# Filler tiles that put nearly every operand of TensorE at 96 modulo 256 bytes of a partition

## The chip, the cores and the metric

The kernel runs on one core of one Trainium2 chip. The metric is the device time of one execution in microseconds (us), the median of three executions.

## What is computed

The input is 16 sequences of 1024 tokens with 512 features, in float32. Each sequence goes through a linear attention block and a feed-forward block, each with a residual sum and a layer norm behind it. The reference, cut to what matters:

```python
# attention: 16 heads of 32
qkv = x @ Wqkv.T + bqkv
q, k, v = split(qkv);  q = rmsnorm(q, gq);  k = rmsnorm(k, gk)
q, k = apply_rope(q), apply_rope(k)
qf, kf = relu(q), relu(k)
vpad = concatenate([v, ones])
vk   = einsum('bhlp,bhld->bhpd', vpad, kf)      # one matrix for a head of a sequence
res  = einsum('bhpd,bhld->bhlp', vk, qf)
attn = res[..., :-1] / (res[..., -1:] + 1e-6)
x = layernorm(x + rmsnorm(attn @ Wout.T + bout, gout))
# feed-forward: mixes each token with the one before it
xr = mu_r * x + (1 - mu_r) * x_prev;  xk = mu_k * x + (1 - mu_k) * x_prev
out = sigmoid(xr @ W_r.T) * (square(relu(xk @ W_k.T)) @ W_v.T)
x = layernorm(x + out)
```

## The kernel before, in words

Tokens go in tiles of 128 (N = 128 tiles, 8 to a sequence). Every float32 matrix product is made of three products: each operand is split in a rounded high part and the rest (`fp32r` tiles named ...h and ...l), and high by high, high by low and low by high are added up in PSUM. Nearly all of TensorE's instructions are therefore pairs of a weight load of 128 x 128 and a matmul with 512 moving columns. In what follows "moving" is the operand that streams (the `rhs` of the code) and "stationary" the one that the weight load reads (`lhsT`).

**Stage A** (slots `slot(i)`, one for each tile, in the first 1250 us or so). `proj` (line 366 on) makes q and k of tile i into `psq` and `psk`: the moving operand is `wqk_h` or `wqk_l`, the stationary one `xh` or `xl`, 12 matmuls each. `add_kx` (line 449) adds x^T k of the tile before into four PSUM banks `pskx`, 12 matmuls: moving `kh` or `kl`, stationary `xnh` or `xnl`. After the eight tiles of a sequence `finish_a` to `finish_c` turn these sums into four matrices m (`pskv` from `kx` by `wa_h` and `wa_l`, `psks` from the key sum, `psm` from `wout_h`, `wout_l` by `kvth`, `kvtl`), which are stored to DRAM.

**Stage B** (the rest). For each tile: `part_qt` transposes q (`psqt`), `part_m` makes the attention output `psy` (moving `mb`, stationary `qth`, `qtl`), and for each block of four tiles `part_t` transposes x (`pst`) and mixes, `part_fk` makes `psk` (moving `mkh`, `mkl`; stationary `w_k`), `part_fr` makes `psr` (moving `w_r`; stationary `mrh`, `mrl`) and `part_fv` makes `psv` (moving `w_v`; stationary `kah`, `kal`). The products of stage B are all emitted by the helper `product` at line 153, 12 matmuls each; the transposes at line 138 use the identity `ident` as moving operand.

The order of the instructions comes from a scheduler that the tile framework runs over the program. It is the same before and after, on every engine and on the DMA queues, and so are all waits.

**Where a tile lies.** SBUF is divided by pools. Pools on the left side grow upwards: `const` first, then `work`, then the pools of the stages (`consta`, `worka`; later `constb`, `workm`, `workb`, `workr`). Pools with `side="right"` grow downwards from the top: `top` first, below it `end`, `endkx`, `endk`; in stage B `workc` takes their place below `top`. A tile's place is its pool's start plus the sizes of the tiles before it, each rounded up to 32 bytes. Nearly all large tiles have a multiple of 2048 bytes in a partition, so the few small tiles ahead of them set where all of a pool begins modulo 256. The addresses of the built program, modulo 256:

| operand of TensorE | pool | before |
|---|---|---|
| `wqk`, `xh`, `xl`; `qth`, `qtl`; `w_k`, `mkh`, `mkl`, `kah`, `kal`; `w_r`, `mrh`, `mrl` | left pools | 96 |
| `mb`, four buffers of six in its ring | `work` (left) | 96 |
| `mb`, the other two buffers; `w_v` | `workc` (right) | 224 |
| `kh`, `kl`, `xnh`, `xnl`; `kx`, `wa`; `wout`, `m` | `endk`, `endkx`, `end` (right) | 192 |
| `ones`, `kvth`, `kvtl` | `end`, behind `bv` and `mask` (right) | 224 |
| `x` (stationary of `pst`), seven buffers in `top`, four in `workc` | right | 224 |
| `q` (stationary of `psqt`) | `top` (right) | 224 |
| `ident` (moving of `pst`, `psqt`) | `const` (left) | 160 |

Of the kernel before, what the change touches and what calls it, by code (L numbers as in the profile page):

```python
# [8 lines left out]
F32 = mybir.dt.float32  # L9
# [6 lines left out]
P = 128  # L16
DIM = 512
NC_ = DIM // P
# [15 lines left out]
def kernel(  # L34
# [34 lines left out]
    const = ctx.enter_context(tc.tile_pool(name="const", bufs=1))  # L69
# [3 lines left out]
    tp = ctx.enter_context(tc.tile_pool(name="top", bufs=1, side="right"))  # L73
# [27 lines left out]
        return pp.tile([P, DIM], F32, tag="mm", bufs=4, name=name)  # L101


    halo = const.tile([P, NC_], F32, name="halo")
    ident = const.tile([P, P], F32, name="ident")
    make_identity(nc, ident)
# [149 lines left out]
    with ExitStack() as a_ctx:  # L256

        te = a_ctx.enter_context(tc.tile_pool(name="end", bufs=1, side="right"))
# [87 lines left out]
            omm[n] = const.tile([P, NC_], F32, name=f"omm_{n}")  # L346
            V.tensor_scalar(omm[n], mu[n], -1.0, 1.0, ALU.mult, ALU.add)

        bv = te.tile([P, NC_], F32, name="bv")
        with nc.allow_non_contiguous_dma(reason="512 numbers"):  # L350
            nc.scalar.dma_start(
                out=bv, in_=bqkv[2 * DIM : 3 * DIM].rearrange("(g p) -> p g", p=P)
# [526 lines left out]
```

## Time and profile before

| | |
|---|---|
| time, median of 3 executions | 2803.57 us (2799.61 to 2805.04) |
| time of the profiled execution | 2802.45 us |
| its span, first to last instruction | 2800.6 us |
| granted TensorE clock over the span | 0.994 of full |
| TensorE matmuls | 12536, busy 2728.1 us (97%) |
| weight loads | 12536, busy 2236.0 us (80%), beside the matmuls |
| VectorE, ScalarE, GpSimd busy | 79%, 68%, 26% |
| DMA | 431.17 MB, mean 154 GB/s |

[...] The chain of work that ended last shows spacings best: a row "start, us, PE, what, x12" is a run of twelve matmuls with nothing between them, and its time divided by twelve is their mean spacing.

### The profile page before, as it was taken

The page shows a single profiled execution, that of the slowest core. Times are in us where ns is not written, and L with a number is a line of the kernel's source. Part 1 is how long each engine was busy: PE and PEld are TensorE (multiplying, and loading weights), DVE is VectorE, ACT ScalarE, POOL GpSimd, SP SyncE. Part 2 cuts the span into 40 slices and gives each one's busy share as a digit, 9 for nine tenths or more (in the row PEclk, how much of TensorE's full clock was granted, in tenths as well). Part 3 has the DMA queues.
Part 4 walks back from the last instruction along what each step waited for, and adds up shares of the span by engine and source line. Part 5 has one row for each costly group of instructions (what it writes and reads, how often), then busy time and mean ns, then how long its engine had stood idle before and what let it go on. Part 6 is the DMA issues. An engine that isn't in the chain of part 4 may idle for free.

```text
span 2800.6 us, 40329 instructions
## 1 busy us (share of the span) xinstructions
PE 2728.1 (97%) x12536; PEld 2236.0 (80%) x12536; DVE 2201.8 (79%) x4966; ACT 1893.1 (68%) x3839; POOL 735.8 (26%) x808
## 2 busy tenths in 40 slices
PE   7999999999999999988999999999999999999998
PEld 5788877777888888866788888888888888888887
DVE  7988877777888788866778787878787878788774
ACT  5566655555555566655777777777777777777775
POOL 6422221221222222222322222222222222222221
PEclk9999999999999999999999999999999999999999
DMA  7787776666777777755323222232323132313210
GB/s 245 234 294 254 236 256 204 213 209 202 231 237 238 237 230 237 231 176 176 104 70 106 95 77 92 92 110 65 106 91 113 57 113 84 110 65 106 76 57 30
DMA packets 230854, 431.17 MB, mean 154 GB/s; under 512 B 24544, under 2 KB 24800, under 8 KB 230640
## 3 DMA queue, kind: packets, MB, share of 16 engines
q1 hardware_dynamic: 228384, 425.85, 46.9%
q10 hardware_dynamic: 2256, 2.76, 0.3%
q8 instruction: 99, 1.62, 0.2%
q14 instruction: 115, 0.94, 0.1%
HBM read 313.14 MB, written 115.38 MB: 153 GB/s over the span
## 4 chain that ended last, share of the span: by engine, by line
PE 76%; DVE 1%; DMA 1%; ACT 1%; issue 0%; POOL 0%; SPq 0%; POOLq 0%; ACTq 0%; DVEq 0%
PE psk L153 13%; PE psv L153 12%; PE psy L153 12%; PE psr L153 12%; PE pskx L462 7%; PE psq L370 7%; PE psk L370 7%; PE pst L138 2%; PE psqt L138 2%; PE psm L538 1%; PE pskv L505 1%; DMA m_d<-m 0%; DMA w_r<-w_dr 0%; PE pskv L513 0%; DMA mb<-m_d 0%
## 5 line engine op out<-in xcount | busy, mean ns | idle before, releaser
L153 PE MATMUL psk<-mkh,w_k 128*128 128x512 f32 x1024 | 337.3, 396 | 0.0
L153 PE MATMUL psr<-w_r,mrh 128*128 128x512 f32 x1024 | 325.9, 400 | 2.6 <-issue 2.6
L153 PE MATMUL psv<-w_v,kah 128*128 128x512 f32 x1024 | 326.4, 400 | 1.5 <-DVE qtl L209 1.5
L153 PE MATMUL psy<-mb,qth 128*128 128x512 f32 x1024 | 319.8, 393 | 2.3 <-ACT qth L208 1.4
L117 POOL TENSOR_TENSOR rstd_all<-ss,mhalf 128x2 f32<-128x2 f32 x128 | 119.1, 931 | 685.6 <-DVE ss L432 666.7
L245 DVE TENSOR_TENSOR y<-psy,g_out 128x512 f32<-128x512 f32 x128 | 88.5, 691 | 187.3 <-PE psy L153 186.6
L370 PE MATMUL psq<-wqk_h,xh 128*128 128x512 f32 x512 | 204.1, 399 | 26.2 <-ACT psq L132 26.2
L153 PEld LDWEIGHTS psy<-mb,qth 128*128 128x128 f32 x1024 | 192.6, 189 | 46.3 <-ACT qth L208 2.2
L153 PEld LDWEIGHTS psk<-mkh,w_k 128*128 128x128 f32 x1024 | 192.3, 188 | 39.4
L153 PEld LDWEIGHTS psr<-w_r,mrh 128*128 128x128 f32 x1024 | 189.5, 190 | 40.1 <-issue 2.8
L153 PEld LDWEIGHTS psv<-w_v,kah 128*128 128x128 f32 x1024 | 187.9, 188 | 41.9 <-DVE qtl L209 1.9
L649 POOL TENSOR_TENSOR mkl<-mixk,mkh 128x512 fp32r<-128x512 f32 x128 | 175.6, 1372 | 150.2 <-ACT mkh L648 150.2
L462 PE MATMUL pskx<-kl,xnh 128*128 128x512 f32 x512 | 203.1, 397 | 5.6 <-DVE kl L439 5.5
L370 PE MATMUL psq<-wqk_l,xh 128*128 128x512 f32 x512 | 203.8, 398 | 0.0
L370 PE MATMUL psq<-wqk_h,xl 128*128 128x512 f32 x512 | 203.7, 398 | 0.0
L462 PE MATMUL pskx<-kh,xnl 128*128 128x512 f32 x512 | 202.2, 395 | 0.0
L153 PE MATMUL psv<-w_v,kal 128*128 128x512 f32 x512 | 202.1, 395 | 0.0
L370 PE MATMUL psk<-wqk_h,xh 128*128 128x512 f32 x512 | 200.4, 391 | 1.8 <-ACT psk L132 1.8
L153 PE MATMUL psy<-mb,qtl 128*128 128x512 f32 x512 | 201.6, 394 | 0.0
L153 PE MATMUL psr<-w_r,mrl 128*128 128x512 f32 x512 | 201.5, 394 | 0.0
L370 PE MATMUL psk<-wqk_h,xl 128*128 128x512 f32 x512 | 200.2, 391 | 0.0
L370 PE MATMUL psk<-wqk_l,xh 128*128 128x512 f32 x512 | 199.8, 390 | 0.0
(148 smaller groups left out, 7248.9 us busy)
## 6 DMA issues: line engine op xcount, KB each, us to landing
tab<-tab_d SPq DMA_DIRECT2D x480, 256.0 KB
xt<-in_xt_dram SPq DMA_DIRECT2D x128, 256.0 KB
xn<-in_x_dram SPq DMA_DIRECT2D x128, 256.0 KB
q_d<-ro SPq DMA_DIRECT2D x128, 256.0 KB
m_d<-m SPq DMA_DIRECT2D x64, 512.0 KB
mb<-m_d SPq DMA_DIRECT2D x64, 512.0 KB
q<-q_d SPq DMA_DIRECT2D x128, 256.0 KB
x<-in_x_dram SPq DMA_DIRECT2D x128, 256.0 KB
```

Of the source, the lines that this page charges most:

```text
L117: G.tensor_tensor(dst, src, mhalf[:, 0 : src.shape[1]], ALU.pow)
L138: T.matmul(ps[:, n * P : (n + 1) * P], lhsT=b, rhs=ident, is_transpose=True, start=(n == 0), stop=(n == NC_ - 1), skip_group_check=True,)
L153: T.matmul(ps, lhsT=a[u][:, rows], rhs=b[w][:, cols], start=(afresh and c == 0 and k == 0), stop=(c == n - 1 and k == 2), skip_group_check ...
L245: V.tensor_mul(y, ps, g_out)
L370: T.matmul(ps, lhsT=a[i][:, c, :], rhs=w_qk[b][:, c, cols], start=False, stop=(c == NC_ - 1 and n == 2), skip_group_check=True,)
L462: T.matmul(ps_kx[b][c], lhsT=a[:, cols], rhs=r, start=(t == 0 and n == 0), stop=(t == 7 and n == 2),)
L505: T.matmul(ps, lhsT=w_a["h"][:, c, cols], rhs=kx[:, c, g, :, :].rearrange("p two n -> p (two n)"), start=(g % 2 == 0 and c == 0), stop=Fal ...
L538: T.matmul(ps, lhsT=a[:, g, :], rhs=w_o[r][:, g, :], start=(n == 0), stop=(n == 2))
L649: (V if n == "r" and s != 1 else G).tensor_sub(ml, m, f32(mh))
```

## The change

Three tiles change their size or are added; none of the three added stretches is ever read or written. In `const` a tile of 256 bytes stands ahead of all others, in `top` one of 128 bytes, and `bv` in `end` grows from 16 bytes (32 with rounding) to 256.

```diff
@@ -101,6 +101,9 @@
+
+    const.tile([P, 64], F32, name="fill_const")
+    tp.tile([P, 32], F32, name="fill_top")
     halo = const.tile([P, NC_], F32, name="halo")
     ident = const.tile([P, P], F32, name="ident")
@@ -346,7 +349,7 @@
-        bv = te.tile([P, NC_], F32, name="bv")
+        bv = te.tile([P, 64], F32, name="bv")[:, 0:NC_]
```

In the built program every tile on the left moves up by 256 bytes and keeps its residue. The tiles of `top` stay at their addresses: the pool's start moves down by 128 bytes and the filler takes these. The pools below `top` start 128 bytes lower; in `end` the tiles ahead of `bv`, and with them all of `endkx` and `endk`, lie 224 bytes lower still. Modulo 256 the operands of TensorE then stand so:

| operand | before | after |
|---|---|---|
| `kh`, `kl`, `xnh`, `xnl`, `kx`, `wa`, `wout`, `m` | 192 | 96 |
| `ones`, `kvth`, `kvtl` | 224 | 96 |
| `w_v`, the two `mb` buffers and the four `x` buffers of `workc` | 224 | 96 |
| all that stood at 96 | 96 | 96 |
| `ident` | 160 | 160 |
| `q`, the seven `x` buffers of `top` | 224 | 224 |

No instruction, order, wait or transfer is added, removed or moved; only addresses differ.

## The prediction

> **What bounds the kernel now.** I read three views in this order: the busy times by stretch, who TensorE waited for, and the chain of work that ended last.
>
> ```profile
> PE 2728.1 (97%) x12536; PEld 2236.0 (80%) x12536; DVE 2201.8 (79%) x4966; ACT 1893.1 (68%) x3839; POOL 735.8 (26%) x808
> PEclk9999999999999999999999999999999999999999
> ...
> 100.00:450.00 350.00, 341.07 (x1547) 279.13 (x1548) 285.38 (x518) 211.80 (x451) 79.62 (x71) 1.00 0.77 250
> 800.00:1000.00 200.00, 200.00 (x920) 165.41 (x919) 166.35 (x303) 120.51 (x260) 44.65 (x41) 1.00 0.74 234
> 2000.00:2700.00 700.00, 700.00 (x3288) 576.82 (x3287) 561.39 (x1502) 536.25 (x1061) 182.23 (x236) 1.00 0.28 89
> ```
>
> TensorE is busy in 97% of the span, in stage A (second window row) as in stage B (last), at full granted clock; VectorE, the next, has 18 to 20% to spare. But busy does not say that TensorE runs at its best spacing. The waits say how little of it is idle:
>
> ```profile
> PE psq L370 <- ACT psq L132: 26.2, 8, 12.7
> PE pskx L462 <- ACT kh L438: 7.8, 6, 1.9
> PE pskx L462 <- DVE kl L439: 5.5, 8, 1.4
> ...
> PE psv L153 <- DVE qtl L209: 1.5, 1, 1.5
> ```
>
> Half of the largest row is the start (one wait of 12.7 us); in stage B the only wait between 1330 and 2800 us is the last row. So the end is set by how densely matmuls follow each other, and the chain shows that they do not do so evenly:
>
> ```profile
> 2760.18 10.90 PE psk L153 x48
> 2771.08 10.88 PE psr L153 x48
> 2781.96 8.41 PE psv L153 x36
> ...
> 2067.03 2.72 PE psy L153 x12
> ...
> 2162.18 2.77 PE psy L153 x12
> ...
> 645.56 2.75 PE psk L370 x12
> 648.30 2.04 PE psq L370 x9
> 650.34 2.77 PE pskx L462 x12
> 653.12 0.70 PE psq L370 x3
> 653.82 2.77 PE psk L370 x12
> ```
>
> Divide time by count. At the end `psk` and `psr` run at 10.88/48 = 226.7 ns, `psv` right behind them at 8.41/36 = 233.6 ns. All three come from the same line with the same shapes. What differs is that `psv` streams `w_v` at 224 modulo 256 against weights at 96, while the two others have 96 on both sides.
>
> **The address is what differs.** From the start times of single matmuls in the trace, each set beside the addresses of the built program, I take three comparisons.
> (1) Within one name: `psy` of tile 72 reads `mb` at 96 alone (2.72 us, spacings 226, 227, 227, 226, 227 and so on), that of tile 80 has two of its four `mb` buffers at 224 (2.77 us; spacings 234, 224, 238, 229, 238, 229 while those last, then 231, 233, 231 and back to 226, 227). Line, weights and neighbours are the same. Other `psy` tiles have their 224 half second, and the slow spacings come second.
> (2) In stage A, `psq` and `psk` are at 96/96, `pskx` at 192/192. Left alone, each of them settles at 226 to 227 ns: 192 is not slow in itself. But where one follows the other there is a spacing of about 237 (192 to 96) or 228 and then, after either, some eight of the kind 229, 233, 236, 224, 231, 236, 228, 232, 231 before it settles. In the fence, `psq` x9 ahead of the crossing has 226.7, `pskx` 230.8, the `psq` x3 behind it 233.
> (3) From `psk` at 96 to `psr` at 96, with tiles far apart in SBUF, nothing is disturbed.
> So I read: a spacing of 226.7 belongs to moving and stationary tile at the same residue; each crossing between residues disturbs the stream for eight or ten matmuls; and a standing difference (`psv`) never lets it settle. That the cause is the residue is inferred, since nothing before varies it alone.
>
> **What the change removes.** No instruction, wait or DMA differs, so no work is added and no queue is passed; the only item is spacing, at fixed counts. I took each 512-column matmul whose spacing is under 245 ns, and replaced it by the mean that undisturbed 96/96 matmuls have at the same distance from the last transpose or stop (transposes disturb the stream too, and stay: `psr` x24 behind them takes 5.49 us, 228.8 ns). Measured against replaced:
> - `psv` 232.7 against 227.9 ns: 4.8 ns x 1472 = 7.0 us.
> - `psy` in stage B: buffers at 224, 232.3 against 226.8 x 442 = 2.4 us; buffers at 96 that recover behind them, 228.2 against 226.8 x 935 = 1.3 us.
> - other products of stage B, 0.2 us. Stage B: 11.0 us.
> - `pskx` 230.9 against 227.3 x 1452 = 5.2 us; `psq` 229.9 against 226.8 x 1475 = 4.5 us; `psk` 228.1 against 227.0 x 1501 = 1.6 us; `psm` 232.5 against 227.0 x 166 = 0.9 us; `psks` and the early `psy`, 0.3 us. Stage A: 12.6 us.
>
> Costed at nothing: the transposes. `ident` keeps 160 and most of their weights keep 224; a set of four takes 0.44 us, 109 ns each, set by weight loads. Should the 176 transposes whose x moves from 224 to 96 change by as much as a crossing's 10 ns, that is under 2 us either way. The `pskv` pairs (0.17 + 0.06 us) are bound by weight loads too: 512 matmuls, 1 us at most. VectorE, ScalarE and GpSimd read other addresses in stage A; no row isolates a residue there. L279 (all tiles at 96) takes 716 ns, L439 (all at 192) 832, L294 (mixed) 819: mixed is no worse than matched, so I take 0, with plus or minus 103 ns on the 128 `kl` of L439 as ends. TensorE's lead hides that; if `kl` came last in every slot it would be 13 us either way. Transfers change only the SBUF address; DMA is busy 0.7 to 0.77 in stage A and 0.28 in B, and hidden.
>
> **What reaches the end.** In stage B nearly all: TensorE waits for nothing, and VectorE is at 561 of 700 us. I take 95%, 10.4 us. In stage A, TensorE needs inputs from VectorE (285 of 350 us busy) and ScalarE chains; between 100 and 1200 us it waited 21 us. What goes from spacing may come back as waits for `psq`'s seed, `kh` or `kl`: they are late next. I take 80%, 10.1 us (ends 30% and 110%, since a shorter stream may also shorten the waits behind it). Sum 20.5 us. The profiled execution took 2802.45 us, so 2782.0; it lies 1.1 us under the median of the runs. I forecast 2783.0 us, 0.7% less.
>
> [...] The rows are 226.7 ns matched and 233.6 ns not. [...] The within-name comparison of `psy` speaks for the rows: the same weights, the same line, 0.05 us of 2.72 us more. [...]
>
> **The rivals.**
> - *Stage A fills with waits* (0.11). The 12.6 us come back as waits for `kh`, `kl` or the seed, stage B keeps its 10.4: 2793. For: VectorE at 81% there, and 26.2 us of seed waits already. Against: windows of 200 us with TensorE fully busy.
> - *The place, not the residue, makes `psv` and `psy` slow* (0.08). All their slow tiles lie in the upper part of SBUF (`workc`); moved by 128 bytes they still do. Stage A's crossings are removed all the same: 2803.6 - 10.1 = 2793.5. Against: 192 to 96 disturbs in the lower part as well.
> - *The change doesn't do what it says* (0.11). What disturbs is the passage from one kind of product to another, and the residue goes along with it by chance; then nothing moves, 2803.6. Against: `psk` to `psr` undisturbed.
> - *Slower: matched tiles of `workc` collide* (0.09). If what counts is the distance between streams in full addresses, `w_v` and `mb` moved against their weights by 384 bytes may land on a worse one: `psv` and the 480 `psy` matmuls then stand at the slow spacing of the trace, 237 to 238, in place of 232.6, 2016 x 5 = 10 us more, with stage A's gain gone to waits: 2813. It decides from a mean `psv` spacing above about 233 without stage A's gain, above about 238 with it. Against: `psr`, at 96/96 with other distances, is clean.
>
> **How the numbers follow.** The main case has 0.61 (2777 to 2790 by the ends of the two shares and a median's scatter), the two half gains 0.19, no effect 0.11, slower 0.09. A measurement of this kernel can tell about 0.2% (5.6 us) from no change. Faster by more: main and both half gains, 0.80; within: 0.11; slower: 0.09. The range from 2777 to 2800 takes in the main case and the half gains, and leaves out no more than the last two.
>
> **What would show it.** Right: in the chain, `psv` x36 at 8.2 us in place of 8.4 (x36 at the very end about 8.16, behind 96/96 without transposes); `psy` x12 at 2.72 for all tiles; in stage A, `pskx` x12 and the `psq` around it at 2.72 to 2.73; stage B some 10 us shorter than before, stage A some 10. Wrong: `psv` still at 232 or more (place or distance, not residue); stage A's pieces at 2.72 but longer rows of waits for L132, L438, L439 (gain turned into waits); L439 or L294 changed in mean by more than 50 ns; any change in the transposes' 0.44.

## The result and the profile after

The changed kernel takes 2784.11 us (median of 6, 2777.75 to 2788.59) against 2802.98 us for the kernel before, run beside it: a ratio of 0.9935, 95% interval 0.992 to 0.9949. A second set on another occasion gave 2781.23 us (median of 5) and 0.9929 (0.9916 to 0.9941). The profiled execution took 2783.7 us with a span of 2781.8.

The page of the kernel after, busy times:

```profile
PE 2707.1 (97%) x12536; PEld 2236.9 (80%) x12536; DVE 2193.8 (79%) x4966; ACT 1886.7 (68%) x3839; POOL 739.3 (27%) x808
```

TensorE's count and share are the same, its busy time is 21 us less, and weight loads and the other engines are where they were, within 8 us: the same work, placed more densely. The waits of TensorE for the seed of `psq` and for `kh` and `kl` (who waits, for whom, us in total, times, longest):

```profile
PE psq L373 <- ACT psq L135: 26.6, 8, 13.0
PE pskx L465 <- ACT kh L441: 9.5, 6, 2.3
...
PE pskx L465 <- DVE kl L442: 3.1, 6, 1.2
```

The sum of these three is 39.2 us, where it was 39.5: no wait has come in place of the time that went. The chain of work that ended last, from the end of the kernel, then from the middle of stage B, then from stage A (start in us, duration in us, what, count; every line number is 3 higher than before, so that line 156 is the 153 of before):

```profile
2741.72 10.88 PE psk L156 x48
2752.60 10.88 PE psr L156 x48
2763.48 8.18 PE psv L156 x36
...
2148.68 2.72 PE psy L156 x12
2151.40 0.44 PE psqt L141 x4
...
2155.05 5.49 PE psr L156 x24
2160.54 2.72 PE psy L156 x12
...
905.02 2.72 PE psq L373 x12
907.74 2.72 PE psk L373 x12
910.46 0.68 PE psm L541 x3
911.14 2.72 PE pskx L465 x12
913.86 2.72 PE psq L373 x12
```

At the end `psv` now runs at 8.18/36 = 227.2 ns (233.6 before). `psr` x24 behind transposes still takes 5.49 us. In stage A products of the left and the right pools follow each other at 2.72 us for twelve, 226.7 ns, with no trace of a crossing; the three `psm` between them take 0.68 us.

Mean spacings in ns from the start times in the trace, each from the start of a matmul to the start of the next (a matmul's own time overlaps the next one: the `psk` matmul at 2154.04 us before takes 389 ns, the next starts 226 ns behind its start). Taken as in the prediction (512 columns, under 245 ns, another such matmul behind):

| | before | foreseen | after |
|---|---|---|---|
| `psv` | 232.7 | 227.9 | 227.6 |
| `psy` of stage B, all | 229.5 | 226.8 | 226.8 |
| `pskx` | 230.9 | 227.3 | 227.5 |
| `psq` | 229.9 | 226.8 | 226.9 |
| `psk` of stage A | 228.1 | 227.0 | 227.0 |
| `psm` | 232.5 | 227.0 | 227.0 |
| `psk`, `psr` of stage B | 228.4, 228.4 | not changed | 228.3, 228.1 |

Since the order is the same, the two traces can be laid beside each other matmul by matmul. Over all spacings that are under 245 ns in both, stage A (up to the first `psk` of stage B) is 12.3 us shorter and stage B 12.0. Over the remaining spacings (waits, stops, half-clock stretches) stage A is 4.3 us longer and stage B 1.2. The net gain is 8.1 us in stage A and 10.7 in stage B.

### The profile page after: what moved, and what is told of

It reads as the page before. It is cut to its first block, busy times and chain, and to the rows that moved or that the text cites. A ratio compares the mean times of both kernels' runs of the same rounds, so it can differ in the third digit from the quotient of the medians.

```text
span 2781.8 us, 40329 instructions
## 1 busy us (share of the span) xinstructions
PE 2707.1 (97%) x12536; PEld 2236.9 (80%) x12536; DVE 2193.8 (79%) x4966; ACT 1886.7 (68%) x3839; POOL 739.3 (27%) x808
## 4 chain that ended last, share of the span: by engine, by line
PE 71%; DVE 2%; DMA 1%; ACT 1%; issue 1%; POOL 0%; SPq 0%; POOLq 0%; ACTq 0%; DVEq 0%
PE psk L156 13%; PE psr L156 12%; PE psv L156 12%; PE psy L156 12%; PE pskx L465 5%; PE psk L373 5%; PE psq L373 5%; PE pst L141 2%; PE psqt L141 2%; PE psm L541 1%; PE pskv L508 1%; DMA m_d<-m 1%; DVE ro L429 0%; DMA mb<-m_d 0%; PE pskv L516 0%
```

## The experiments

All of them change fillers alone; order and work are those of the two kernels above. "Shorter" below is against the kernel before, matmul by matmul, the dense part (spacings under 245 ns in both traces) by itself. Differences of residues are moving minus stationary, modulo 256.

**One half alone.** Stage A's right-hand tiles:

```diff
# kernel before
-        bv = te.tile([P, NC_], F32, name="bv")
+        bv = te.tile([P, 32], F32, name="bv")[:, 0:NC_]
```

> Only the tiles of stage A's right-hand pools that are read as kh, kl, xnh, xnl, kx, wa, wout and m go from 192 to 96; w_v and two mb buffers stay at 224, kvth, kvtl and ones too. Residue theory (matched residues settle at 226.7 ns, a mismatch disturbs): pskx, psq and psk of stage A at 227 to 227.5 ns mean spacing, psv still 232.7 and psy with its 224 buffers 232.3; stage A 7 to 9 us shorter, stage B unchanged, time 2794 to 2796 against 2803. Rival, the passage between kinds of product disturbs whatever the addresses are: spacings of stage A as before, time 2803.

Measured: 2796.76 us, ratio 0.9982 (0.9975 to 0.999). `pskx` 227.7, `psq` 227.6, `psk` 227.2; `psv` 232.7 as before. The dense part of stage A is 8.9 us shorter, that of stage B unchanged (0.2 us longer). Stage A's spacings went as the residue theory says; 3.4 of the changed kernel's 12.3 us are missing. `kvth` and `kvtl` stayed at 224, and their products `psm`, now at 96 against 224, went from 227.0 in the changed kernel to 236.1 ns: 1.5 us for 166 of them; the rest fits the matmuls behind them that they disturb (`psq` 227.6 against 226.9, `psk` 227.2 against 227.0), which was not tested apart. The time came 1 to 3 us above what was expected. In the profiled execution, 5.4 us were lost outside the dense part of stage B, at the passage from stage A, in part to longer stops (a wait for `mb` took 3.1 us, 0.9 before); whether the other executions lost as much is not known.

Stage B's tiles:

```diff
# changed kernel, whose other two fillers stay
-        bv = te.tile([P, 64], F32, name="bv")[:, 0:NC_]
+        bv = te.tile([P, 40], F32, name="bv")[:, 0:NC_]
```

With this size `wout`, `m`, `wa`, `kx`, `kh`, `kl`, `xnh`, `xnl` come out at 192 as before.

> Only w_v, two mb buffers and four x buffers go from 224 to 96 (and kvth, kvtl, ones); stage A's 192 tiles stay. Residue theory: psv at 227.6 to 228, psy at 226.8, pskx still 230.9 and psq 229.9; stage B 10 to 11 us shorter, time 2792 to 2793 against 2803. Rival, place (the upper part of SBUF is slow): psv stays at 232 or more and the time at 2803. The two halves should add up to the whole change within 2 us if nothing links the stages.

Measured: 2790.43 us, 0.9954 (0.9943 to 0.9966). `psv` 227.6, `psy` 226.7; `pskx` 231.2, `psq` 229.5. Dense part: stage B 11.8 us shorter, stage A 0.3. The chain's end:

```profile
2745.73 10.88 PE psk L156 x48
2756.61 10.88 PE psr L156 x48
2767.49 8.17 PE psv L156 x36
```

The tiles moved by 128 bytes within the upper part of SBUF and the slow spacing is gone, so the upper part is not what made it slow. The halves give 5.5 and 11.8 us of the medians, 17.3 together; the whole gave 18.9 and 21.

**Is it 96, or equality?** Everything that stands at 96 is put at 0:

```diff
# changed kernel
-    const.tile([P, 64], F32, name="fill_const")
-    tp.tile([P, 32], F32, name="fill_top")
+    const.tile([P, 104], F32, name="fill_const")
+    tp.tile([P, 56], F32, name="fill_top")
```

> All that stands at 96 modulo 256 in the changed kernel stands at 0 here (left pools up by another 160 bytes, right pools down by 96); ident at 64, q and seven x buffers at 224. If only the equality of the residues counts: 2784 within 3 us, psv 227.6, pskx 227.5, each settling at 226.7. If 96 itself is a good value (an absolute start within some line), spacings settle elsewhere: above 227 for all products would be over 2 us for each ns (some 11000 spaced matmuls are 11 us for each ns), so 2795 or more at 227.7.

Measured: 2780.28 us, 0.992 (0.9907 to 0.9933). `psv` 228.0, `pskx` 227.4, `psq` 226.8; the dense part 24.8 us shorter, against 24.3 with 96. Equality counts, not 96. The chain's end:

```profile
2740.72 10.88 PE psk L156 x48
2751.60 10.88 PE psr L156 x48
2762.48 8.17 PE psv L156 x36
```

This kernel also bears on the 256. In its built program `w_v` stands 256 bytes off its weights modulo 512, and all of stage A's right-hand tiles stand at 256 modulo 512 beside 0 on the left; neither shows in the spacings (`psv` 228.0 here, and 227.5 in the last kernel below, which has the same offsets). No cost shows at a difference of 256, while one of 128 has 232.7 (`psv` before), so the period is 256 here and no longer.

**The transposes too.** `ident`, `q` and the `x` buffers of `top` are put at 96 as well:

```diff
# changed kernel
-    const.tile([P, 64], F32, name="fill_const")
-    tp.tile([P, 32], F32, name="fill_top")
+    const.tile([P, 48], F32, name="fill_const")
     ident = const.tile([P, P], F32, name="ident")
+    const.tile([P, 16], F32, name="fill_const2")
...
         for i in range(N):
             slot(i)
+        tp.tile([P, 32], F32, name="fill_top")     # behind the pool's own tiles: these move down
```

> The changed kernel with ident, q and the x buffers of the top pool at 96 as well (the filler of the top pool put behind its tiles, that of the first pool split around ident). Theory 1, what still disturbs the stream behind transposes is the residue of ident (160) and of q and x (224): then psk, psr, psv of stage B go from 228.3, 228.1, 227.6 to about 226.8, some 5 us less, and psr or psy ahead of a transpose from 231 to 227: 2778 to 2780. Theory 2, the disturbance comes from the transposes being bound by their weight loads (109 ns each), with no backlog of loads left: unchanged, 2784 within 2 us, transposes still 109 ns.

Measured: 2785.08 us, 0.9932 (0.9919 to 0.9944). The products of stage B have 227.5 for `psr` (228.1 in the changed kernel), 228.2 for `psk` (228.3) and 227.5 for `psv` (227.6); the last matmul ahead of a transpose stays at 232.3, and transposes at 109.4. The dense part gains 0.8 us over the changed kernel. Theory 1 fails and the time is as theory 2 has it: what is left of the disturbance comes with the transposes whatever their addresses, which carry under 1 us. That their weight loads are the reason, as theory 2 says, was not tested apart.

**The other place.** In the changed kernel `w_r`, on the left, in the lower part of SBUF, is put off its weights by 128:

```diff
         own["ks"] = wr
+        wr.tile([P, 32], F32, name="fill_wr")
```

> The changed kernel with 128 bytes of filler ahead of w_r in its left-hand pool: w_r at 224 against its weights at 96, all else at 96. Residue theory: psr goes from 228.1 to 232 to 233.7 ns, with psv and psy behind it slightly up as they recover; stage B 7 to 8 us longer than the changed kernel, time 2791 to 2792. Place theory (only the upper part of SBUF is slow): psr stays at 228.1, time 2784.

Measured: 2789.65 us, 0.9951 (0.9936 to 0.9967). `psr` 232.7, `psv` 228.0, `psy` 227.8; the dense part of stage B 9.0 us longer than in the changed kernel. In the chain now the product at fault is the other one:

```profile
2746.45 10.88 PE psk L156 x48
2757.33 11.19 PE psr L156 x48
2768.52 8.19 PE psv L156 x36
```

11.19/48 = 233.1 ns for `psr`, and `psv` behind it back at 227.5. 128 bytes of filler make either product slow or fast (`psr` 232.7 or 228.1, `psv` 232.7 or 227.6), in either part of SBUF. The time came 1.4 us below the expected one.

**How far off is how bad?** The changed kernel with the filler of `top` cut from 128 bytes to 96, to 64 and to none moves all right-hand operands to 128, 160 and 224:

```diff
-    tp.tile([P, 32], F32, name="fill_top")
+    tp.tile([P, 24], F32, name="fill_top")     # 32 off; [P, 16] for 64 off; no tile for 128 off
```

> As the changed kernel, but with 96 in place of 128 bytes of filler in the top pool: all right-hand operands stand at 128, 32 bytes off the 96 of the left. Theory 1, any difference modulo 256 disturbs alike: psv at 232 to 233.7, pskx 230 to 231, psq 229 to 230, time 2800 to 2804. Theory 2, only the line of 64 or 128 bytes matters: 96 and 128 lie in different lines of 64 and of 128, so disturbed as well, but with 64 bytes off (next run) as well. Theory 3, the cost grows with the difference: psv at 228.5 to 229.5, time about 2788. Rival, place: changed kernel's 227.6 with any residue.

Measured: 2802.26 us, 0.9998 (0.9989 to 1.0008). `psv` 233.2, `pskx` 229.5, `psq` 229.3.

> The same with 64 bytes of filler: right-hand operands at 160, 64 off. Theory 1: psv 232 to 233.7 and 2800 to 2804, as with 32 and 128 off. If the period were 64 bytes: clean, psv 227.6, 2784; the trace of before (128 off, disturbed) speaks against that. Theory 3: between the 32 and the 128 bytes off, psv 230 to 231, time about 2793.

Measured: 2796.46 us, 0.9976 (0.9965 to 0.9987). `psv` 229.7, `pskx` 229.7, `psq` 228.7.

> The same with no filler in the top pool: all right-hand operands at 224, 128 off, in stage A too. psv and psy as before the change (232.7; buffers at 224 at 232.3). Residue theory: pskx and psq of stage A disturbed as with 192, 229.5 to 231. Time 2802 to 2805. If 192 and 96 were special: stage A clean, 2794.

Measured: 2796.64 us, 0.9981 (0.9971 to 0.999). `psv` 232.7, as expected; but `pskx` 228.4 and `psq` 227.8: the dense part of stage A is 8.4 us shorter than with its tiles at 192 (96 off), and the time 5 us below the expected one. The chains' ends, 32, 64 and 128 off in this order:

```profile
2783.29 8.42 PE psv L156 x36
```
```profile
2775.84 8.27 PE psv L156 x36
```
```profile
2774.79 8.41 PE psv L155 x36
```

None of the three theories holds: the cost is not the same for all differences (64 off: 229.7), and it does not grow with them (32 off is worse than 64). And what a difference costs while it stands (`psv`) is not what crossing it costs (`pskx`): 128 off is among the dear ones standing (`psv` 232.7), and the cheapest to cross (`pskx` 228.4). The traces show where that comes from. Averaged over some 90 crossings from `psq` or `psk` to `pskx`, a crossing of 128 is over after two spacings (232.4, 231.1, then 227 to 228); one of 96, in the kernel before, takes about ten (229.5, 234.7, 233.1, 234.6, 227.0, 230.2, 233.0, 229.1, 231.2, 230.4). In the changed kernel the same places stand at 226.6 to 226.8.

**The rest of the differences.** A filler ahead of `w_r` and one behind all tiles of `workc` (which moves these down) set two more in one kernel:

```diff
# changed kernel; second version: [P, 48] and [P, 8]
         own["ks"] = wr
+        wr.tile([P, 24], F32, name="fill_wr")
...
                         load_ks(j // 8 + 1)
+    wc.tile([P, 24], F32, name="fill_wc")
```

> The changed kernel with w_r at 192 (96 bytes ahead of its weights modulo 256) and workc at 0 (w_v and two mb buffers 160 ahead), to read the standing spacing of two more differences. Known so far: 0 gives 226.7, 32 ahead 233.2, 64 ahead 229.7, 128 ahead 232.7 (psv) and 232.7 (psr). If the cost grows with the distance from the nearest multiple of 256, psr at 96 and psv at 160 stand alike, at 231 to 233, time about 2796. If odd multiples of 32 are the bad ones, both at 233 or more, time 2797 to 2800. If the sign matters (moving ahead of or behind the weights), the two differ by over 1 ns.

Measured: 2803.02 us, 1.0009 (0.9999 to 1.0019). `psr` 233.3 at 96 ahead, `psv` 233.9 at 160:

```profile
2769.72 11.21 PE psr L156 x48
2780.93 8.45 PE psv L156 x36
```

The time is higher than expected, because the two `mb` buffers of `workc` are off as well and `psy` goes to 230.2.

> The same with w_r at 32 (192 ahead, or 64 behind) and workc at 64 (224 ahead, or 32 behind). If the cost is the same for ahead and behind: psr at 229.7 as with 64 ahead, psv at 233.2 as with 32 ahead. If the sign matters, either is off by over 1 ns. Time 2790 to 2796.

Measured: 2802.62 us, 1.0001 (0.999 to 1.0011). `psr` 233.4 at 192 ahead, `psv` 233.1 at 224. So 64 behind is not 64 ahead: 233.4 against 229.7. This compares `psr` with `psv`; at 128, the one difference at which both were measured, they agree (232.7). Between 32 ahead and 32 behind `psv` shows none (233.2, 233.1). The time is more than 6 us above the expected one, `psy` being off here too (230.2). The chain's end:

```profile
2771.49 11.20 PE psr L156 x48
2782.69 8.41 PE psv L156 x36
```

**All at 0, and the changed kernel again.** `ident`, `q` and all `x` buffers at 0 too:

```diff
# changed kernel
-    const.tile([P, 64], F32, name="fill_const")
-    tp.tile([P, 32], F32, name="fill_top")
+    const.tile([P, 24], F32, name="fill_const")
     ident = const.tile([P, P], F32, name="ident")
+    const.tile([P, 80], F32, name="fill_const2")
...
         for i in range(N):
             slot(i)
+        tp.tile([P, 56], F32, name="fill_top")
```

> Every operand of TensorE at 0 modulo 256, ident, q and all x buffers too: the version that the runs so far point to. Dense spacing can save about 1 us over the changed kernel (behind transposes psr 227.5 in place of 228.1 was seen with all at 96); 2779 to 2783. If 0 is better than 96 for something beside spacing (transfers into SBUF, other engines), 2780 as the kernel with all but the transposes at 0; if that one's 2780.3 was scatter, 2784.

Measured: 2780.17 us, 0.9927 (0.9913 to 0.994); the dense part gains 0.5 us over the changed kernel.

> The changed kernel as it is, on the same chip as the one with all at 0: 2784 within 3 us. If it comes within 2 us of the kernel at 0, then 0 and 96 are the same and the difference between 2784.1 and 2780.3 was scatter.

Measured: 2781.23 us, 0.9929 (0.9916 to 0.9941), 1.1 us from the kernel at 0. The 3.8 us between the first medians of 96 and 0 were scatter; no version measured can be told to be faster than the changed kernel.

## Why the prediction was right

The forecast was 2783.0 us; 2784.1 and 2781.2 were measured. By its steps:

- **What bounds the kernel.** Right: the density of TensorE's stream. Its spacings fell and the end came forward with them, while weight loads, waits and the other engines stayed as they were.
- **The address as the cause**, inferred there. Shown by the runs: `psv` 232.7 to 227.6 by moving the tiles of `workc` (the run of stage B's tiles), `psr` 228.1 to 232.7 by moving `w_r` alone, and the same times at 96 and at 0. Had the addresses cost nothing, the time would have stayed at 2803.6; 2784.1 was measured. How the two operands lie to each other is not free here: the differences measured, 32 to 224 bytes, cost 2 to 6 ns for each matmul.
- **The size of the spacing term.** 23.6 us foreseen, 24.3 measured in the dense part (12.6 against 12.3 in stage A, 11.0 against 12.0 in stage B). It came out so closely because the undisturbed 96/96 spacing, at each distance from the last transpose or stop, stood in the trace of before, and because in the changed kernel no mismatch among the 512-column matmuls is left.
- **The transposes at nothing.** Right: 0.44 us for four before and after, and with matched transposes 109.4 ns for each. That weight loads set it, and the `pskv` pairs too, is the author's reading, which no run tests apart. The trace of before agrees with it: the loads of a set of transposes start 109 ns apart as well (2154.73, 2154.84 and 2154.95 us), the two loads of a `pskv` pair 109 ns (median), and the 128-column matmul of that pair has the next one 59 ns behind its start.
- **The other engines at nothing.** Right as far as the bounds go: the mean of L439 (now L442) went from 832 to 827 ns, that of L294 (L297) from 819 to 843, within the 50 ns allowed. Their medians stand within 1 ns (count, shortest, median and longest in ns; before, then after):

```profile
L439 DVE TENSOR_TENSOR kl<-ro,kh x128: 672/683/1816, 37.9 to 1239.0; 128x512 fp32r<-128x512 f32 x128
L294 DVE TENSOR_TENSOR xnl<-xn,xnh x128: 674/686/1772, 20.6 to 1230.1; 128x512 fp32r<-128x512 f32 x128
...
L442 DVE TENSOR_TENSOR kl<-ro,kh x128: 673/684/1824, 37.7 to 1230.9; 128x512 fp32r<-128x512 f32 x128
L297 DVE TENSOR_TENSOR xnl<-xn,xnh x128: 674/685/1783, 20.9 to 1222.0; 128x512 fp32r<-128x512 f32 x128
```

  The means lie above the medians because 23 to 27 of the 128 instances take over 1 us, up to 1.8. L294 has 23 of these and L297 27, which makes most of its 24 ns more; its tiles went from mixed residues to one and the same, and the median did not move.
- **What reaches the end.** Stage B: 10.4 foreseen, 10.7 measured. Stage A: 10.1 foreseen; 8.1 in the first profiled execution, 11.5 in the second of the same kernel, of a dense 12.3 and 12.0. The size came out, the reason only in part, and so this term owes something to luck: the gain was expected back as waits for the seed, `kh` and `kl`, but those three rows sum to 39.5 us before and to 39.2 and 37.3 in the two executions. What took part of it in the first execution is the clock. In short stretches, mostly of 3.4 us, the profile shows a granted clock of 0.5, and `psq`, `psk` and `pskx` stand at 427 ns. They recur at nearly the same places, but which of them an execution has varies. Between 50 and 1200 us before has four (78, 412, 515, 679 us), the first execution of the changed kernel six (57, 77, 408, 511, 593, 675), the second five (56, 408, 428, 510, 592). Half of 3.4 us is lost in each, so the first lost an estimated 3.4 us more to them than before, of the 4.3 by which its other spacings are longer. Other kernels with matched tiles in stage A have 7.3 to 10.9 us of a dense 12.3 to 12.5, against the same one trace of before. The share of 80% is close to their average, and single executions stray from that by some 2 us.

The rivals: that the place in SBUF is at fault, and that the passage between kinds of product is, are excluded by the kernels above; stage A's gain was not turned into waits; the collision in `workc` did not come. Its price, `psv` standing at 237 to 238 ns, was seen at no difference either: the dearest is 233.9. What the prediction left open is that mismatches do not all cost the same; it did not enter the sum, since all mismatches among the 512-column matmuls are removed.

## What to carry to other kernels

When TensorE is busy all the time, read its spacing (a chain piece's time by its count) for each product: two products of the same shape with different spacing are a reason to look where their operands lie. In a stream of weight load and matmul pairs as here, begin the streamed and the stationary tile at the same byte modulo 256 (`psv` 227.6 ns, against 229.7 to 233.9 off it), and let neighbouring products keep that residue (`pskx` 227.5 ns, against 230.9 between products at another). A small tile at the head of a pool can shift everything behind it; here fillers of at most 256 bytes mended it. A gain in spacing is worth its full count only where nothing else stops the stream: 12.0 us gave 10.7 here in stage B, and in stage A 12.3 gave 8.1 in one execution and 12.0 gave 11.5 in another; part of it varies with stops and clock.

## What the runs showed of the hardware

Mean spacing of 512-column `fp32r` matmuls, each with its own weight load, by how far the moving tile's first byte stands ahead of the stationary tile's, modulo 256:

| difference | 0 | 32 | 64 | 96 | 128 | 160 | 192 | 224 |
|---|---|---|---|---|---|---|---|---|
| `psv`, ns | 227.6 | 233.2 | 229.7 | | 232.7 | 233.9 | | 233.1 |
| `psr`, ns | 228.1 | | | 233.3 | 232.7 | | 233.4 | |

I had not expected that 64 bytes ahead costs only 2 ns where 64 behind costs 5, nor that the cost of a standing difference and that of crossing one are ordered differently (stage A's dense part, against the changed kernel: 12.3 us at 96 off, of which 0.9 is the standing mismatch of `psm`, then 7.9 at 32, 6.7 at 64, 3.9 at 128, where the standing order is 233.3, 233.2, 229.7, 232.7 ns).

The crossings say one thing more. There both products are matched in themselves, and still the stream is disturbed. In the trace the weight load of the next matmul runs while a matmul streams (before, a load starts at 2059.13 us beside the `psk` matmul that started at 2059.12), so at a crossing the stream of one product and the weight load of the next stand at different residues. It may be this meeting that costs, and not the pair within one matmul; no run separates the two, since in a standing mismatch both differ. Why residues matter at all is open: nothing in the traces shows the reads inside SBUF. Also open is whether it holds for matmuls of other types or widths, which were not tried.
